# An adaLN block on one core: a written engine order up to the first h2, section steps one by one, four PSUM buffers for the first y, two warm-up matmuls

## The chip, the core and the metric

The kernel runs on one core of a Trainium2 chip. Its time is the device time of one execution in microseconds (us). A core has five engines that work side by side: TensorE (PE, matmul), VectorE (DVE), ScalarE (ACT), GpSimd (POOL) and SyncE (SP), which here only issues DMAs. Each engine works through its own instruction stream in order and waits on semaphores for the others. DMAs are issued from SP's stream, and one of them from ACT's.

## What is computed

x is (2, 2048, 1024) in float32: two batch entries of 2048 tokens with 1024 channels. From the reference, cut to what matters:

```python
mod = (_silu(L0_c) @ L0_wmod).reshape(2, 6, 1, -1)
sa, ca, ga, sb, cb, gb = (mod[:, 0], mod[:, 1], mod[:, 2], mod[:, 3], mod[:, 4], mod[:, 5])
ga = (2 * (ga >= 0) - 1) * jnp.maximum(jnp.abs(ga), 0.25)       # gb likewise
h = _layernorm(x, axis=-1) * (1 + ca) + sa
x = x + ga * attn(h)
h = _layernorm(x, axis=-1) * (1 + cb) + sb
return x + gb * ffn(h)

# attn: for each channel l a 2x2 softmax over the batch entries
q = jnp.transpose(x, (2, 0, 1))
prob = softmax(jnp.einsum('lnc,lmc->lnm', q, q) / scale)
return x + jnp.transpose(jnp.einsum('lnm,lmc->lnc', prob, q), (1, 2, 0))

# ffn: FF = 2752
y = (_silu(xf @ W_gate.T) * (xf @ W_up.T)) @ W_down.T
```

The attention needs, for each channel, sums over all 2048 tokens of z, of z squared and of the product of the two batch entries, where z is the normalised x. So there is one pass over all of x before anything else can begin.

## The kernel before

Tokens are worked in eight units of 256 (both batch entries together). Behind the pass over x each unit computes its y, the second layernorm (its result is called h2), the two projections to FF (gate and up, in pairs of 128-row blocks of FF), and the projection back. Float32 operands are split into a high and a low float16 part, and three of the four products are summed (`PARTS`). Units 1 to 7 form the projections as two-by-two block products in seven steps; unit 0 uses the plain product `gu_plain`, because its weights are split and written back to DRAM while it runs.

What comes before unit 0's first product, and some way into it, is the stretch that the change touches, from 0 to about 160 us. Its parts in order:

- **Modulation sections** 0 to 4 (`sa`, `ca`, `ga`, `sb`, `cb`). A section j has four loads of 1 MiB (`mod_load`, L158, DMA to `hbt`, `H` or `wt`; called w0 to w4 here), four steps of four matmuls (`mod_mul`, L165), a copy of the sum out of PSUM (`mod_row`, L171), a turn by four matmuls (`mod_turn`, L177) and a copy to SBUF (`mod_put`, L185/L187).
- **The pass over x**: `x_step` (L321) for eight steps of 256 tokens. It computes statistics and 1/std (`stats`, `root`, `dev`), z on DVE, POOL and ACT (`z_of`, L282), the products on POOL (L337), the squares on ACT (L318), and sums all of them by matmuls against a selector (`add`, L308, into the PSUM tile `sums`). It also transposes unit 0's z (`x_turn`, L299; `x_turned`, L304).
- `stat_rows` (L285 to L292) turns mean and 1/std of all tokens (PE, L289), copies them to SBUF (ACT, L291) and writes them to DRAM with a DMA that ACT issues (L292); unit 1's preparation reads them there.
- **The attention weights** alpha and beta from the sums (L1116 to L1149): a row copy (ACT), `pq` (PE, L1118), some thirty small DVE operations, an Exp and a dummy Sqrt on ACT, which loads the function table ahead of its use, and section 2.
- `first_y` (L648 to L662): for each of eight channel blocks q two activations `po` (ACT, L657), two products with z (DVE, L659), the addition to x (POOL for even q, DVE for odd, L660), and a matmul that sums over channels (`pmean`, L661). `po` is a PSUM tile of tag X, of which there are two.
- `first_dev` (L664 to L676): minus the mean (DVE, L668), squares (ACT, L671), sums `pvar` (PE, L673). `first_spread` (L679) is 1/std of the 128 x 128 result; `spread` (L683) lays it over all partitions (`pr`, L686).
- `first_h2` (L690 to L705): for each block two products with `pr` (DVE, L699), the high half (ACT, L701) and the low half (DVE), and between the blocks the four `split`s of pair 0's weights (L128: high half on POOL or ACT, low half on DVE). Pair 0's weights need their own power-of-two scale, from sums of squares (L115) by `pow2_from_sumsq` (L98) and `over_partitions` (L90).
- `gu_plain` (L739) for p = 0, 1, 2, ...: in p = 0 four warm-up matmuls (`WARM`, L749), then for each of four blocks i the products (L759).

Who sets the order: inside `tc.manual_schedule` an engine's instructions stand in the order of the text. SP is under it from the start to the last load of pair 0 (`in_order`). PE, DVE, ACT and POOL are under it (`in_text`) only for the pass over x, up to `in_text.close()` ahead of `mod_put(0, ...)`. What follows is placed by a scheduler that simulates time; `tc.issue_after(m)` keeps an instruction behind the marked one. The section steps are given such marks: section 2's stand after the sums of steps 6 and 7 and after pq, section 3's after the last `pmean`, section 4's after some of the `pvar` sums. Pair p's four float32 weight blocks are loaded by `Pair.load` (L412): pair 0 to `H`, pair 1 to `rot`, pair 2 to `big`. On SP's queue the order there is w2, w3, w4, pair 0, pair 1, pair 2 (four loads each).

Of the kernel before, what the change touches and what calls it, by code (L numbers as in the profile page):

```python
# [47 lines left out]
def adaln_kernel(ctx, tc, x, xT, wgp, wg20, wgl, wd, wd20, wd21, wmod, cT, out, nunits=NU):  # L48
# [41 lines left out]
    def over_partitions(col):  # L90

        pa = ps.tile([P, P], F32, tag="st", name="pa")
        mark["row"] = T.matmul(pa, col.broadcast_to([P, P]), ident, start=True, stop=True)
        a = small.tile([P, 1], F32, tag="p2a", name="p2a")
        V.tensor_reduce(a, pa, AX.X, ALU.max)
        return a


    def pow2_from_sumsq(col, s, inv):
        b = small.tile([P, 1], F32, tag="p2b", name="p2b")  # L100
        V.tensor_scalar(b, col, 1e-30, 1e38, ALU.max, ALU.min)
        a = over_partitions(b)
# [3 lines left out]
        V.tensor_single_scalar(inv.bitcast(I32), c, 0x1A000000, ALU.add)  # L106

# [9 lines left out]
    def rsqrt(dst, v, shape, pool, tag):  # L117

        s = pool if tag is None else pool.tile(shape, F32, tag=tag, name=tag + "s")
        first = S.activation(s, v, AF.Sqrt, bias=epst)  # L120
# [5 lines left out]
        return first, V.scalar_tensor_tensor(dst, s, 1.5, dst, ALU.add, ALU.mult)  # L126

    def split(dst_hi, dst_lo, src, s, on_pool=False):  # L128
        if on_pool:
            G.tensor_scalar(dst_hi, src, s, 0.0, ALU.mult, ALU.add)  # L130
        else:
            mark["hi"] = S.activation(dst_hi, src, AF.Copy, scale=s)  # L132
        return V.scalar_tensor_tensor(dst_lo, src, s, dst_hi, ALU.mult, ALU.subtract)  # L133
# [58 lines left out]
    def mod_section(j, slots, tag):  # L192
# [5 lines left out]
        mod_end(j, pm, tag)  # L198

    def section_of(j, wms, tag, after=None):  # L200

        pm = ps.tile([P, 512], F32, tag=tag, name=f"pm{j}")
        for kk, wm in enumerate(wms):
            with tc.issue_after(after[kk].ins) if after else ExitStack():
                mod_mul(pm, kk, wm)
        mod_end(j, pm, tag)
# [114 lines left out]
    def x_step(s):  # L321
# [11 lines left out]
        z_of(G, s, 1, 0)  # L333
        for n in range(2):
            z_of(S, s, n, 1)
        for c in range(NC):
            G.tensor_tensor(zz_at[c], z[c][0], z[c][1], ALU.mult)  # L337
# [4 lines left out]
        if s:  # L342
            turned[s - 1] = x_turn(z_first, s - 1)
            x_turned(zt, s - 1, turned[s - 1], S)
# [5 lines left out]
        for c in range(NC):  # L350
            add(s, 2, 2 * c, zz_at[c])
        for n in range(2):
            add(s, 1, 2 * n, zq[2 + n])
# [46 lines left out]
    class Pair:  # L400
# [15 lines left out]

        def scale(self):
            scale_of(self.sq, self.s, inv_gu[:, self.p:self.p + 1])
# [4 lines left out]
        def block(self, i, keep=True):  # L423
            w = self.w[i] = wtile(2 * self.n, "wq")
            split(w[:, 0:self.n], w[:, self.n:], self.q[i], self.s, on_pool=i % 2 == 1)
            if keep:
                self.store(i)
# [44 lines left out]
    WARM = 4  # L472
# [87 lines left out]
    def mod_b(mx1):  # L560

        b1 = mods[4]
        mx = small.tile([P, 1], F32, tag="mx", name="mx")
        V.tensor_reduce(mx, b1.rearrange("p k n -> p (k n)"), AX.X, ALU.max, apply_absolute_value=True)
        V.scalar_tensor_tensor(mx, mx, 33.0, mx1, ALU.mult, ALU.add)
        ma = over_partitions(mx)
        mark["mod_row"] = mark["row"]
# [4 lines left out]
        for n, src in (("b1", b1), ("sb", mods[3])):  # L572
# [75 lines left out]
    def first_y():  # L648
# [4 lines left out]
        for q in range(KB):  # L653
            po = ps.tile([P, 2, TU], F32, tag="X", name="po")
            o = tmp.tile([P, 2, TU], F32, tag="o", name="o", bufs=3) if q % 2 == 0 else po
            for n in range(2):
                mark["o"] = S.activation(po[:, n], zt[:, q, 0], AF.Identity, scale=alpha[:, n, 0, q:q + 1],  # L657
                                         bias=beta[:, n, q:q + 1])
                V.scalar_tensor_tensor(o[:, n], zt[:, q, 1], alpha[:, n, 1, q:q + 1], po[:, n], ALU.mult, ALU.add)  # L659
            (G if q % 2 == 0 else V).tensor_tensor(x0[:, q], o, x0[:, q], ALU.add)  # L660
            mark["y", q] = T.matmul(pm, ones, xf0[:, q], start=q == 0, stop=q == KB - 1)  # L661
        return pm  # L662

    def first_dev(pm):  # L664
        nb = 2 * TU // P
        pv = ps.tile([P, P], F32, tag="st", name="pvar")
        for q in range(KB):
# [3 lines left out]
            mark["sq"] = S.activation(sq, zf0[:, q], AF.Square)  # L671
            for j in range(nb):
                mark["var", q] = T.matmul(pv[32 * j:32 * j + 32], ones[:, 0:32], sq[:, j * P:(j + 1) * P], start=q == 0,  # L673
                                       stop=q == KB - 1, skip_group_check=True)
        mark["pv"] = pv

    def first_spread():
        rs = evp.tile([P, 512], F32, tag="ev", name="rs", bufs=3)[:, 0:P]
        mark["rv"], mark["rs"] = rsqrt(rs, mark["pv"], [P, P], ps.tile([P, P], F32, tag="X", name="rv"), None)  # L679
        return rs  # L680

    def spread(rs):
        nb = 2 * TU // P  # L683
        pr = ps.tile([P, 2 * TU], F32, tag="st", name="pr")
        for j in range(nb):
            mark["pr"] = T.matmul(pr[:, j * P:(j + 1) * P], ident[:, 32 * j:32 * j + 1].broadcast_to([P, P]), rs, start=j == 0,  # L686
                     stop=j == nb - 1, skip_group_check=True)
        return pr

    def first_h2(pr, blocks):  # L690
        h0 = hb0.rearrange("p h k (n c) -> p h k n c", n=2)
        b1s, sbs = mods["b1"], mods["sb"]
        with tc.manual_schedule(engines={mybir.EngineType.DVE}):
            for q in range(KB + 1):
                if q in blocks:
                    pairs[0].block(blocks[q], keep=False)
                for n in range(2):
                    if q < KB:
                        V.scalar_tensor_tensor(zt[:, q, n], zt[:, q, n], b1s[:, q, n:n + 1], pr[:, n * TU:(n + 1) * TU],  # L699
                                               ALU.mult, ALU.mult)  # L700
                        mark["h2"] = S.activation(h0[:, 0, q, n], zt[:, q, n], AF.Identity, bias=sbs[:, q, n:n + 1])  # L701
                for n in range(2):
# [528 lines left out]
```

## Time and profile before

| | us |
|---|---|
| median of 3 runs shown | 2629.77 (2627.58 to 2632.89) |
| the profiled execution | 2636.85 |
| its span, first to last instruction | 2635.1 |
| mean granted TensorE clock, of 1 | 0.992 |
| PE busy | 2563.4 (97%) |
| DVE busy | 1587.8 (60%) |
| ACT busy | 986.3 (37%) |
| POOL busy | 129.8 (5%) |

Points on the way to unit 0, from the timeline of the profiled execution:

| | at us |
|---|---|
| last `sums` matmul ends | 82.97 |
| stat DMA issued by ACT | 83.08 |
| beta ready, first `po` of first_y | 92.95, 92.98 |
| first `dev` of first_dev | 106.91 |
| first product of h2 | 124.09 |
| first matmul of `gu_plain`, p = 0, on PE | 127.56 |
| first matmul of p = 1 | 155.01 |
| first matmul of p = 2 | 178.26 |

How to read it: the page's table of slices cuts the span into 40 equal parts of 65.9 us and gives a digit of busy share for each engine. A row of the timeline gives start, duration, engine, line, operation, out<-in with shape, how many instructions follow one another without a gap, and in square brackets the engine's idle time before them and who ended it. A DMA's row on SP or ACT is its issue; the list of DMA issues gives the time from there to its landing. The granted clock is what the chip's throttle gave PE in a window.

### The profile page before, as it was taken

What the parts mean: (1) busy time and instruction counts of PE and PEld (TensorE: products, weight loads), DVE (VectorE), ACT (ScalarE), POOL (GpSimd) and SP (SyncE); (2) the same over time, 40 slices, a digit from 0 to 9 for tenths busy, and PEclk for the clock granted to TensorE, in tenths of its full rate; (3) what the DMA queues carried; (4) which work ended last, traced back from release to release, by engine and by line L of the source; (5) the groups of instructions that cost most, each with busy time, mean ns of one, the idle gap of its engine ahead of it and who ended that gap; (6) DMA issues with size and microseconds to landing.
All of it is one profiled execution on the core that took longest, in us unless ns stands there. A gap on an engine that the chain in (4) does not pass through costs nothing.

```text
span 2635.1 us, 50643 instructions
## 1 busy us (share of the span) xinstructions
PE 2563.4 (97%) x21673; PEld 2088.9 (79%) x21673; DVE 1587.8 (60%) x2648; ACT 986.3 (37%) x1502; POOL 129.8 (5%) x70
## 2 busy tenths in 40 slices
PE   7899999999999999999999999999999999999999
PEld 2344458788887888888887888878887888888887
DVE  8567779856676877583385625574284825622263
ACT  7677664433432444142242423233141513311230
POOL 6211100000000000000000000000000000000000
PEclk9999999999999999999999999999999999999999
DMA  9888765655568766576666666576666666656664
GB/s 391 315 307 309 309 245 187 228 201 192 171 202 295 249 232 203 195 239 200 194 208 219 208 200 200 197 229 201 191 214 211 210 202 201 202 192 203 202 199 152
DMA packets 159009, 586.61 MB, mean 223 GB/s; under 512 B 17216, under 2 KB 17280, under 8 KB 158784
## 3 DMA queue, kind: packets, MB, share of 16 engines
q1 hardware_dynamic: 158704, 583.35, 66.5%
q8 instruction: 169, 2.77, 0.4%
q14 instruction: 56, 0.46, 0.1%
q10 hardware_dynamic: 80, 0.03, 0.0%
HBM read 506.47 MB, written 76.84 MB: 221 GB/s over the span
## 4 chain that ended last, share of the span: by engine, by line
PE 79%; DMA 8%; DVE 7%; issue 3%; ACT 2%; POOL 0%; SPq 0%; DVEq 0%; ACTq 0%; POOLq 0%
PE pY L816 19%; PE pZ L816 12%; PE pX L816 12%; PE dY L1020 11%; PE dX L1020 8%; PE dZ L1020 7%; PE g L784 3%; PE pB L1046 3%; PE pl L854 1%; DMA wo<-dgu 1%; ACT junk L115 1%; DMA rot<-in_wgp_dram 1%; DVE bst L256 1%; DMA rot<-in_wd_dram 1%; PE g L759 1%
## 5 line engine op out<-in xcount | busy, mean ns | idle before, releaser
L816 PEld LDWEIGHTS <-w 128*128 128x128 f16 x8820 | 861.5, 98 | 109.6 <-DMA w<-dgu 6.9
L1020 PEld LDWEIGHTS <-wd 128*128 128x128 f16 x6720 | 658.3, 98 | 81.2 <-DMA wd<-dwd 4.0
L816 PE MATMUL pY<-hbt,w 128*128 128x256 f16 x3780 | 442.4, 273 | 0.0
L1020 PE MATMUL dY<-rot,wd 128*128 128x256 f16 x2880 | 320.3, 273 | 0.0
L816 PE MATMUL pX<-hbt,w 128*128 128x256 f16 x2520 | 300.6, 273 | 0.0
L816 PE MATMUL pZ<-hbt,w 128*128 128x256 f16 x2520 | 294.4, 273 | 5.8 <-DMA w<-dgu 5.0
L816 PEld LDWEIGHTS <-wo 128*128 128x128 f16 x2688 | 263.4, 98 | 39.4 <-DMA wo<-dgu 4.6
L132 ACT ACTIVATE rot<-H,sA 128x1024 f16<-128x1024 f32 (+1 forms) x168 | 162.7, 1001 | 239.7 <-PE dY L1020 129.8
L133 DVE SCALAR_TENSOR_TENSOR rot<-H,sA,rot 128x1024 f16<-128x1024 f32 (+1 forms) x168 | 182.2, 1100 | 80.3 <-ACT rot L132 80.0
L759 PE MATMUL g<-hbt,wq 128*128 128x512 f16 x1008 | 221.0, 379 | 2.7 <-ACT hbt L701 2.1
L1020 PE MATMUL dX<-rot,wd 128*128 128x256 f16 x1920 | 212.7, 273 | 3.7 <-DMA wd<-dwd 3.7
L1020 PE MATMUL dZ<-rot,wd 128*128 128x256 f16 x1920 | 213.5, 273 | 0.0
L833 DVE TENSOR_TENSOR ev<-pY,e 128x512 f32<-128x512 f32 (+1 forms) x72 | 47.8, 663 | 257.5 <-PE pY L816 256.5
L759 PEld LDWEIGHTS <-wq 128*128 128x128 f16 x1008 | 98.3, 98 | 120.7 <-issue 3.4
L115 ACT ACTIVATE junk<-H 128x1024 bf16<-128x1024 f32 (+1 forms) x100 | 98.7, 987 | 160.1 <-DVE H L843 139.1
L838 ACT ACTIVATE sil<-ev,inv_f 128x512 f32<-128x512 f32 (+1 forms) x72 | 50.4, 701 | 242.8 <-DVE ev L836 242.5
L816 PE MATMUL pY<-hbt,wo 128*128 128x256 f16 x1152 | 134.7, 273 | 2.6 <-DVE ev L833 2.4
L613 ACT ACTIVATE o<-big,beta,alpha 128x256 f32<-128x256 f32 x112 | 59.9, 591 | 203.4 <-DVE big L599 181.1
L824 DVE TENSOR_TENSOR ev<-pY,e 128x512 f32<-128x512 f32 (+1 forms) x72 | 47.7, 663 | 124.0 <-PE pY L816 124.0
L784 PE MATMUL g<-hbt,wo 128*128 128x256 f16 x960 | 108.0, 275 | 4.8 <-DMA wo<-dgu 4.8
L827 ACT COPY e<-pZ 128x512 f32<-128x512 f32 (+1 forms) x72 | 40.4, 562 | 190.1 <-PE pZ L816 189.9
L784 PEld LDWEIGHTS <-wo 128*128 128x128 f16 x960 | 94.3, 99 | 17.9 <-DMA wo<-dgu 5.7
(286 smaller groups left out, 2731.9 us busy)
## 6 DMA issues: line engine op xcount, KB each, us to landing
w<-dgu SPq DMA_DIRECT2D x350, 512.0 KB, 4.3
wd<-dwd SPq DMA_DIRECT2D x224, 640.0 KB, 4.0
wo<-dgu SPq DMA_DIRECT2D x85, 512.0 KB, 5.2
dgu<-wo SPq DMA_DIRECT2D x40, 512.0 KB, 4.1
rot<-in_wgp_dram SPq DMA_DIRECT2D x38, 512.0 KB, 6.0
dgu<-wq SPq DMA_DIRECT2D x35, 512.0 KB, 7.0
big<-in_wgp_dram SPq DMA_DIRECT2D x32, 512.0 KB, 8.0
out_dram<-big SPq DMA_DIRECT2D x30, 512.0 KB, 3.0
```

What stands on the lines that cost most here:

```text
L115: S.activation(jv, src, AF.Square, accum_out=col)
L132: mark["hi"] = S.activation(dst_hi, src, AF.Copy, scale=s)
L133: return V.scalar_tensor_tensor(dst_lo, src, s, dst_hi, ALU.mult, ALU.subtract)
L613: S.activation(o[:, n], z[:, q, 0], AF.Identity, scale=alpha[:, n, 0, q:q + 1], bias=beta[:, n, q:q + 1])
L759: T.matmul(pt[m, f].rearrange("p n c -> p (n c)"), w[:, wa, f, k], hb0[:, ha, 4 * kh + k], start=kh == 0 and k == 0 and j == 0, stop=kh == ...
L784: T.matmul(pt[m, f][:, n], w[:, wa, f, k], hb[:, ((1, 0), (2, 3))[kh][n], ha, k], start=kh == 0 and k == 0 and j == 0 and n == 0, stop=kh ...
L816: T.matmul(pt[a][:, f], w[:, wa, f, k], hb[:, i, ha, k], start=a not in seen, stop=k == 3 and j == 2, skip_group_check=True)
L824: V.tensor_tensor(u2, pt["Y"], e1, ALU.add)
L833: V.tensor_tensor(c22, pt["Y"], e1, ALU.add)
L838: S.activation(sr, u2, AF.Silu, scale=inv)
L1020: T.matmul(acc[a, h][:, j], w[:, k // 5, wa, k % 5], rot16[:, si % 2, ha, k], start=(a, h) not in seen, stop=k == KH - 1 and jj == 2, skip ...
L1046: T.matmul(pB, wt[0:n, k, wa, m, :], hp[0:n, k, ha, :], start=i == 0, stop=i == len(LAST) - 1)
```

## The change

The written order (`in_text`, and `in_order` for SP) is carried on from the pass over x to the end of the first h2. The code there is put into the order in which it is to run; the marks that stood in for it go. In detail:

- **Section steps one by one.** Section 0's four steps stand behind x-steps 2 and 3 as before; its turn moves from behind the pass to behind step 5, where section 1's first two steps stand too; section 1's last two stand inside step 6, ahead of its last four `add` matmuls (`between`). Section 2's four steps stand together behind pq. Section 3's stand behind q = 2, 3, 5 and 6 of first_y, with its row, turn and `mod_put` behind q = 7, followed by three of pair 0's sums of squares and section 4's first two steps; section 4's third and fourth step stand behind q = 2 and 4 of first_dev.
- **Step 7 of the pass**: the two z's of the second 128 tokens and the second product move from ACT and POOL to DVE; the transposes of blocks 6 and 7 stand both in it, ahead of the sums, and DVE copies them.
- **stat_rows** moves from behind the pass to just ahead of first_y.
- A dummy Exp ahead of pq loads the function table.
- **first_y**: `po` alternates between PSUM tags X and Y, four buffers instead of two.
- **first_h2** is cut in two halves, and pair 0's splits are cut into `high` (blocks 0, 1 and 3 on POOL, 2 on ACT) and `low` (DVE). DVE's order is: eight products of h2, low 0, eight lows of h2, eight products, low 1, eight lows, low 2, low 3. Pair 1's sums of squares and scale stand between and behind them, ahead of unit 0.
- **gu_plain**: `WARM` is 2 instead of 4, and in p = 0 the first two blocks' products are sorted by part (high by high, low by high, high by low); before it was the first block alone, sorted in the order of `PARTS`.

On SP's queue the order becomes: w2, w3's first two, pair 2's four (`big`), w3's last two, pair 0's four, w4's four, pair 1's four. ACT's stream gets the stat DMA directly ahead of the first `po`. Behind about 160 us the two builds have the same order but for some swaps.

The diff, cut to its core:

```diff
-    def x_step(s):
+    def x_step(s, between):
 
         z = [[z_tiles(s)[n][:, c] for n in range(2)] for c in range(NC)]
         if s == 0:
@@ -331,17 +335,18 @@
         if more:
             stats(s + 1, 1)
         z_of(G, s, 1, 0)
+
         for n in range(2):
-            z_of(S, s, n, 1)
+            z_of(S if more else V, s, n, 1)
         for c in range(NC):
-            G.tensor_tensor(zz_at[c], z[c][0], z[c][1], ALU.mult)
+            (G if more or c == 0 else V).tensor_tensor(zz_at[c], z[c][0], z[c][1], ALU.mult)
         zq = squares(s, 0)
         if more:
             root(s + 1)
         zq += squares(s, 1)
-        if s:
-            turned[s - 1] = x_turn(z_first, s - 1)
-            x_turned(zt, s - 1, turned[s - 1], S)
+        for k in range(s - 1, s + 1 - more):
+            if k >= 0:
+                x_turned(zt, k, x_turn(z_first, k), S if more else V)
         for c in range(NC):
             for n in range(2):
                 add(s, 0, 2 * n, z[c][n])
@@ -349,6 +354,7 @@
             add(s, 1, 2 * n, zq[n])
         for c in range(NC):
             add(s, 2, 2 * c, zz_at[c])
+        between()
         for n in range(2):
...
-    WARM = 4
+    WARM = 2
...
-    def first_y():
+    def first_y(between):
 
 
         x0 = xtile(0)
         pm = ps.tile([P, 2 * TU], F32, tag="st", name="pmean")
         for q in range(KB):
-            po = ps.tile([P, 2, TU], F32, tag="X", name="po")
+            po = ps.tile([P, 2, TU], F32, tag="XY"[q % 2], name="po")
             o = tmp.tile([P, 2, TU], F32, tag="o", name="o", bufs=3) if q % 2 == 0 else po
             for n in range(2):
-                mark["o"] = S.activation(po[:, n], zt[:, q, 0], AF.Identity, scale=alpha[:, n, 0, q:q + 1],
-                                         bias=beta[:, n, q:q + 1])
+                S.activation(po[:, n], zt[:, q, 0], AF.Identity, scale=alpha[:, n, 0, q:q + 1], bias=beta[:, n, q:q + 1])
                 V.scalar_tensor_tensor(o[:, n], zt[:, q, 1], alpha[:, n, 1, q:q + 1], po[:, n], ALU.mult, ALU.add)
             (G if q % 2 == 0 else V).tensor_tensor(x0[:, q], o, x0[:, q], ALU.add)
-            mark["y", q] = T.matmul(pm, ones, xf0[:, q], start=q == 0, stop=q == KB - 1)
+            T.matmul(pm, ones, xf0[:, q], start=q == 0, stop=q == KB - 1)
+            between(q)
         return pm
 
...
+    def first_h2(pr, qs):
+        for q in qs:
+            for n in range(2):
+                V.scalar_tensor_tensor(zt[:, q, n], zt[:, q, n], mods["b1"][:, q, n:n + 1], pr[:, n * TU:(n + 1) * TU],
+                                       ALU.mult, ALU.mult)
+                mark["h2"] = S.activation(h0[:, 0, q, n], zt[:, q, n], AF.Identity, bias=mods["sb"][:, q, n:n + 1])
+
+    def first_h2_low(qs):
+        for q in qs:
+            for n in range(2):
+                V.scalar_tensor_tensor(h0[:, 1, q, n], zt[:, q, n], mods["sb"][:, q, n:n + 1], h0[:, 0, q, n],
+                                       ALU.add, ALU.subtract)
...
-            if p == 0 and i == 0:
-                fkj.sort(key=lambda t: t[2])
+            if p == 0 and i < 2:
+                fkj.sort(key=lambda t: (0, 2, 1)[t[2]])
...
+    def steps_of(j, ws, kks):
+        if 0 in kks:
+            pms[j] = ps.tile([P, 512], F32, tag="st" if j < 2 else "Z", name=f"pm{j}")
+        for kk in kks:
+            mod_mul(pms[j], kk, ws[kk])
+
+    def row_of(j):
+        rows[j] = mod_row(j, pms[j])
+
+    def turn_of(j):
+        pts[j] = mod_turn(j, rows[j], "st" if j < 2 else "Z")
+
     for g in range(NU):
-        x_step(g)
+        def between():
+            if g == 6:
+                steps_of(1, w1, (2, 3))
+
+        x_step(g, between)
         if g + 4 < NU:
             x_load(g + 4)
         if g == 0:
             w0 += [mod_load(0, kk, slots[0:4]) for kk in (2, 3)]
-        for j, ws, g0 in ((0, w0, 2), (1, w1, 5)):
-            if g == g0:
-                pms[j] = ps.tile([P, 512], F32, tag="st", name=f"pm{j}")
-            if g0 <= g < g0 + 2:
-                for kk in (2 * (g - g0), 2 * (g - g0) + 1):
-                    mod_mul(pms[j], kk, ws[kk])
         if g in (2, 3):
+            steps_of(0, w0, (2 * g - 4, 2 * g - 3))
             w1 += [mod_load(1, kk, slots[0:4]) for kk in (2 * g - 4, 2 * g - 3)]
         if g == 4:
-            rows[0] = mod_row(0, pms[0])
-    x_turned(zt, KB - 1, x_turn(z_first, KB - 1), V)
-    in_text.close()
-    mod_put(0, mod_turn(0, rows[0], "st"))
-    mod_end(1, pms[1], "st")
-    stat_rows()
-
-
-    sa, ca = mods[0], mods[1]
+            row_of(0)
+        if g == 5:
+            turn_of(0)
+            steps_of(1, w1, (0, 1))
+    w2 = [mod_load(2, kk, slots_x) for kk in range(4)]
+    w3 = [mod_load(3, kk, slots[0:4]) for kk in range(4)]
+    pairs[0].load()
+    row_of(1)
+    turn_of(1)
+    mod_put(0, pts[0])
...
     row = evp.tile([P, 512], F32, tag="ev", name="srow", bufs=3)
     S.copy(row, sums_ps)
+    dummy = small.tile([P, 1], F32, tag="dum", name="dum", bufs=1)
+    S.activation(dummy, epst, AF.Exp)
     for b in range(4):
-        mark["pq"] = T.matmul(pq[:, b], row[:, b * P:(b + 1) * P], e10, start=b == 0, stop=b == 3, skip_group_check=True)
+        T.matmul(pq[:, b], row[:, b * P:(b + 1) * P], e10, start=b == 0, stop=b == 3, skip_group_check=True)
+    steps_of(2, w2, range(4))
+    w4 = [mod_load(4, kk, slots_x) for kk in range(4)]
+    pairs[1] = Pair(1, four(rot))
+    pairs[1].load()
...
-    ex = S.activation(Zz, Zz, AF.Exp, scale=float(NTOK) ** -0.5)
-    dummy = small.tile([P, 1], F32, tag="dum", name="dum", bufs=1)
-    with tc.issue_after(ex.ins):
-        S.activation(dummy, epst, AF.Sqrt)
+    S.activation(Zz, Zz, AF.Exp, scale=float(NTOK) ** -0.5)
+    row_of(2)
+    turn_of(2)
+    S.activation(dummy, epst, AF.Sqrt)
     V.tensor_tensor(mx, Zz[:, :, 0], Zz[:, :, 1], ALU.add)
     V.reciprocal(mx, mx)
     V.tensor_tensor(Zz, Zz, over_m(mx), ALU.mult)
     V.tensor_tensor(Zz, Zz, eye, ALU.add)
-    w2 = [mod_load(2, kk, slots_x) for kk in range(4)]
-    section_of(2, w2, "Z", [mark["sums", 6], mark["sums", 7], mark["pq"], mark["pq"]])
+    mod_put(2, pts[2])
     gate(mods[2])
     V.tensor_tensor(Zz, Zz, bn(mods[2]), ALU.mult)
     V.tensor_tensor(alpha, Zz, bm(a1), ALU.mult)
     V.tensor_tensor(us, Zz, bm(sa), ALU.mult)
     V.tensor_tensor(beta, us[:, :, 0], us[:, :, 1], ALU.add)
-    w3 = [mod_load(3, kk, slots[0:4]) for kk in range(4)]
-    w4 = [mod_load(4, kk, slots_x) for kk in range(4)]
-    pairs[0].load()
+    stat_rows()
+
+
+    def in_y(q):
+        if q in (2, 3, 5, 6):
+            steps_of(3, w3, [(2, 3, 5, 6).index(q)])
+        if q == KB - 1:
+            row_of(3)
+            turn_of(3)
+            mod_put(3, pts[3])
+            for i in (0, 2, 3):
+                pairs[0].sums(i)
+            steps_of(4, w4, (0, 1))
+
+    pm = first_y(in_y)
+    mx1 = mod_b_shift()
+
+    def in_dev(q):
+        if q in (2, 4):
+            steps_of(4, w4, [1 + q // 2])
+        if q == 5:
+            row_of(4)
+            turn_of(4)
+
+    pv = first_dev(pm, in_dev)
+    rs = evp.tile([P, 512], F32, tag="ev", name="rs", bufs=3)[:, 0:P]
+    rv = ps.tile([P, P], F32, tag="X", name="rv")
+    mod_put(4, pts[4])
+    pb = mod_b_start(mx1)
+    S.activation(rv, pv, AF.Sqrt, bias=epst)
+    pairs[0].sums(1)
+    V.reciprocal(rs, rv)
+    V.scalar_tensor_tensor(rv, pv, EPS, rs, ALU.add, ALU.mult)
+    mod_b_end(pb)
+    pp = pairs[0].scale_start()
+    V.scalar_tensor_tensor(rv, rv, -0.5, rs, ALU.mult, ALU.mult)
+    V.scalar_tensor_tensor(rs, rv, 1.5, rs, ALU.add, ALU.mult)
+    pairs[0].scale_end(pp)
+    for i in range(2):
+        pairs[0].high(i, True)
+    pr = spread(rs)
+    pairs[0].inv()
+    first_h2(pr, range(4))
+    pairs[0].low(0)
+    first_h2_low(range(4))
+    for i in (0, 2):
+        pairs[1].sums(i)
+    first_h2(pr, range(4, KB))
+    pairs[0].high(2, False)
+    pairs[0].high(3, True)
+    for i in (3, 1):
+        pairs[1].sums(i)
+    for i in range(1, 4):
+        pairs[0].low(i)
+        if i == 1:
+            first_h2_low(range(4, KB))
+    pairs[1].scale()
+    pairs[1].inv()
+    in_text.close()
     in_order.close()
-    ctx.enter_context(tc.issue_after(mark["load"].ins))
-    pm = first_y()
-    section_of(3, w3, "Z", [mark["y", KB - 1]] * 4)
-    first_dev(pm)
-    with tc.issue_after(mark["sq"].ins):
-        for i in (0, 2, 3, 1):
-            pairs[0].sums(i)
-    section_of(4, w4, "Z", [mark["var", 1], mark["var", 3], mark["var", 7], mark["var", 7]])
-    mod_b(mod_b_shift())
-    rs = first_spread()
-    pairs[0].scale()
-    pr = spread(rs)
-    with tc.issue_after(mark["rv"].ins):
-        first_h2(pr, {1: 0, 3: 1, 5: 2, 7: 3})
-    pairs[0].inv()
-    with tc.issue_after(mark["h2"].ins):
-        pairs[1] = Pair(1, four(rot))
-        pairs[1].load()
-        for i in range(4):
-            pairs[0].store(i)
-        for i in range(4):
-            pairs[1].sums(i)
-        pairs[1].scale()
-        pairs[1].inv()
+    ctx.enter_context(tc.issue_after(mark["h2"].ins))
+    for i in range(4):
+        pairs[0].store(i)
     for u in range(nunits):
         last = u + 1 == nunits
         unit(u, iter(()) if last else prep(u + 1), None if last else right_gu(V))
```

## The prediction, made before the changed kernel was run

> **What bounds the kernel now.** I read the table of slices first, then the clock and load of the first 150 us in windows of 5 us, then the waits of SP's queue, then each engine's timeline there.
>
> ```profile
> span 2635.1 us, 50643 instructions
> PE   7899999999999999999999999999999999999999
> PEclk9999999999999999999999999999999999999999
> DMA  9888765655568766576666666576666666656664
> ```
>
> One digit is 65.9 us. From the fourth on PE is full; only the first two to three leave something to win. The change reorders work before about 160 us, and the built order behind that differs in a handful of swaps. So I walk that stretch and ask how much earlier or later it hands over to unit 0's second pair (p=2), from where PE is busy without a pause. The profiled execution took 2636.85 us (span 2635.1); the median shown is 2629.77, 7.1 below. I sum on the profiled one and put the difference on the median. About 0.2% (5.3 us) is what a measurement of this kernel can tell from no change.
>
> ```profile
> 85.00:90.00 5.00, 4.29 (x36) 2.35 (x32) 1.80 (x14) 1.66 (x2) 0.00 (x0) 1.00 0.91 303
> 90.00:95.00 5.00, 0.01 (x1) 0.00 (x0) 3.46 (x17) 3.88 (x8) 0.00 (x0) 0.84 1.02 392
> 95.00:100.00 5.00, 3.41 (x4) 1.46 (x5) 4.52 (x10) 3.63 (x8) 2.54 (x2) 0.50 1.03 419
> 100.00:105.00 5.00, 4.39 (x10) 1.56 (x9) 3.77 (x8) 3.13 (x6) 2.54 (x2) 0.98 1.03 409
> ```
>
> (Window, length, then busy us of PE, PEld, DVE, ACT, POOL, granted clock, DMA share, GB/s.) Two things bear on the change: the loads fill the DMA engines (share 1.0) to 110 us, so a load moved back lands later; and PE, idle from 90.0 to 96.6, comes back at half clock (0.50).
>
> ```profile
> 83.08 0.51 ACTq L292 DMA_DIRECT2D stat<-hp  x1
> 92.98 2.81 ACT L657 ACTIVATE po<-big,beta,alpha 128x256 f32<-128x256 f32 x5 [1.02 <-DVE beta L1149]
> SPq L412 <- DMA hbt<-in_wmod_dram: 6.5, 4, 2.5
> ```
>
> SP's row says that loads of a pair waited four times, 6.5 us in all, for w4's loads to land. They write other buffers; what they share is a place eight DMAs on. In the trace the `rot` loads issue at 93.83, 97.11 and 99.19, just after w4's at 93.75, 96.63 and 99.18 landed; so do the next four after theirs. So in this program a DMA waits for the one eight before it. The stat DMA of L292 follows that rule and sits in ACT's own stream: at 83.08 its partner, w2's first load, had landed (68.82), and it cost nothing.
>
> **Part 1, the pass over x and the sums: gain.** Step 7 moves two z's and one product to DVE, whose rows are 0.81 (z) against 1.24 on ACT and 1.73 on POOL; the second POOL product (2.39, ends 78.85) leaves. hs, mod and eye work leave DVE's order ahead of step 7's dev, which comes 2.45 earlier. pt1 (0.95) and p16 (0.28) leave PE ahead of the last sums. PE then runs through from 65 us with 15.1 of work: the last sums end at 80.1 instead of 82.97.
>
> **Part 2, to alpha and beta: gain 3.9, then lost.** pq ends 2.1 after the sums instead of 3.4 (p16's and pz's place is free), and the Exp table load (1.28 at 88.92) is hidden by the dummy Exp. But w2's 16 matmuls (3.5) now follow pq in one go, then row 0.57 and turn 1.05; these end last. beta is ready at 89.1 instead of 92.95.
>
> **Part 3, the new wait: the largest term.** stat_rows now stands behind beta and just ahead of first_y. In the built order its DMA is number 49, and number 41 is w4's first load. That load is moved back too: before, it follows w3; after, the four `big` loads of pair 2 stand between w3's halves and pair 0's four loads ahead of w4. Durations on the full queue: 2.56 for 1 MiB, 1.28 for 512 KB. Before, w2's last lands at 76.48, w3's last at 87.53, w4's first at 91.22, pair 0's 100.46 to 104.30, pair 1's to 109.42, pair 2's to 114.44. After: w3's first two 82.4, pair 2's four 87.6, w3's other two 92.7, pair 0's four 97.8, **w4's first 100.4**. From the other end: pair 0's second landing, 101.74, less the 1.1 us gap before w4 that goes, is 100.6. I take 100.5. Behind the waiting DMA on ACT stand all 16 activations of first_y, and behind those DVE, POOL and PE. First po: 100.5 + 0.1 + issue 0.5 = 101.1, against 92.98: **8.1 later**. If the wait did not hold ACT: 89.1.
>
> **Part 4, first y.** Four PSUM buffers instead of two take out the gaps of DVE (0.64, 0.25, 0.15, 0.25, 0.64): 16 x 0.49 + 4 x 0.69 = 10.6, to 112.4, against 13.0 now. What is late next is PE: q=0 arrives over POOL (1.27) at 104.0; then eight pmean passes at 0.86 and four steps of w3, four matmuls each, also 0.86, which before ran behind the mean (106.80 to 110.4): 12 x 0.86 = 10.3.
>
> ```profile
> 95.26 1.27 POOL L660 TENSOR_TENSOR big<-o,big 128x512 f32<-128x512 f32 x1 [16.42 <-DVE o L659]
> 96.59 7.31 PE L661 MATMUL pmean<-big,ones 128*128 128x512 f32 x12 [6.57 <-POOL big L660]
> 106.91 4.87 DVE L668 TENSOR_TENSOR big<-big,pmean 128x512 f32<-128x512 f32 x8 [1.22 <-PE pmean L661]
> ```
>
> The 6.57 of idle on the PE row is followed by the clock of 0.50, and the first four records there last 0.85 instead of 0.43: +1.7. I add 1.7 to 2.4 and take 2.0: mean at 116.3. From below, nothing is possible only if PE did not idle, but after the change it idles from about 88 to 104, longer than before. [...]
>
> **Part 5, dev to the first h2: gain.** pt3 (turn 1.05) and mod3 with its maximum (0.57) now stand on DVE ahead of dev: dev starts at 117.9 (106.91 before, +11.0). ACT puts row3 and three sums of squares (1.18 each) ahead of the eight squares, to 119.55; the squares (0.52 each) and row4 (0.57) run to 125.3, held by w4's third step. Then var 0.3, square root 0.32, reciprocal 0.96, three products 0.3 each with the small operations between, rs 129.3, pr 2.07.
>
> ```profile
> 120.00:125.00 5.00, 4.26 (x16) 3.09 (x16) 2.93 (x18) 2.24 (x3) 2.01 (x2) 0.66 0.56 195
> 124.09 0.87 DVE L699 SCALAR_TENSOR_TENSOR big<-big,b1s,pr 128x256 f32<-128x256 f32 x2 [0.91 <-PE pr L686]
> ```
>
> First h2 at 131.65 against 124.09: from dev 13.7 instead of 17.1, since the sums of squares and row4 no longer stand between the squares and rs. **+7.6** here.
>
> **Part 6, unit 0's first pair.** The lows and h2's go 8 by 8 on DVE: 32 x 0.395 + 4 x 1.2 = 17.4, before 17.6. High blocks on POOL (1.12) instead of ACT (1.14): even. Two warm-up matmul pairs instead of four take 1.8 off 3.65; PE waits for DVE here, so this costs nothing at warm clock, and if the clock stayed half the bound is the 1.7 of the row above. PE ends the pair at 157.9 (151.04 before): +6.9. The second pair then saves: its scale is already done, so PE's pauses of 1.73 and of the `pa` waits up to 155.01 go, as does part of the 1.92 of a section step. First matmul of p=2: 182.6 instead of 178.26. **Sum: +4.3, with swaps +4.5**; 2636.85 + 4.5 = 2641.4, or 2634.3 on the median's scale.
>
> **The rivals.**
> - *No hold on ACT* (faster): the stat DMA passes, first_y starts at 89.1, and the 12.0 us come off everything up to h2: 4.5 - 12.0 = -7.5, **2622.3**. For it: in the trace of before this very DMA never waited. Against: its partner had landed by then, and the `rot` loads did wait. Chance 0.10.
> - *Clock* (slower): PE idles 16 us, so first_y and the tail stay at half clock longer. One window more costs 1.7 (+6.2, 2636); the whole of first_y cold costs 6.9, some of it under DVE (to 2641). It decides from 0.8 us beyond my sum. For it: 0.50 after 6.57 idle. Against: 0.98 in the next window. **2637.5**, chance 0.27.
> - *A later wait swallows the delay*: the chain of waits from 184 us on goes through the loads of `wd`. They issue only some 2 us later than before (158.95 against 156.95), so if that chain, not PE, sets unit 0, the delay shrinks to 0 to +2. For it: DMA is 8% of the chain that ended last. Against: PE is full in those slices. **2630.5**, chance 0.18.
> - *Forecast*: 2634.3 (own range 2631.5 to 2637), chance 0.45.
>
> **How the numbers follow.** Faster by over 0.2% is only the first rival: 0.10. The bound on the slow side is 2629.77 + 5.3 = 2635.1. Slower takes the clock's 0.27 but for 0.03, and 0.17 of the forecast's 0.45, whose upper end passes the bound: 0.41. Same: 0.49. The range leaves out the first rival and the cold extreme: 2626 to 2641.
>
> **What would show it.** In the profile after: the stat DMA on ACT's queue issues at 100 to 101 with w4's first load landing just ahead, and the first po follows within 1 us; DVE has no gap between the products of first y; PE's granted clock is 0.5 around 104; the first dev starts near 118, the first h2 near 132, p=2's first matmul near 182.6. If the first po stands near 89, part 3 is wrong; if p=2 starts at 182 and the end is not later, the third rival holds.

## The result, and the profile after

The changed kernel takes 2643.92 us (median of 5, 2639.84 to 2647.07) against 2630.87 (median of 5, 2627.58 to 2632.89) for the kernel before: ratio 1.0048, 95% interval 1.0033 to 1.0063. Measured a second time beside other kernels, 2643.53 against 2635.96, ratio 1.0028 (1.0017 to 1.0039). It is slower by 0.3 to 0.5%, 7 to 13 us. The forecast was 4.5 us slower, range 2626 to 2641: the time lies above the range.

The profiled execution took 2647.07 us. Its first lines and the table of slices:

```profile
span 2645.1 us, 50642 instructions
...
PE   7699999999999999999999999999999999999999
...
PEclk9899999999999999999999999999999999999999
DMA  9778875665467776676666666676666666656664
```

Only the second slice (66 to 132 us) is worse: PE 6 instead of 8, clock 8 instead of 9. From the third on PE is as full as before. So the place is where the forecast put it. The windows of the changed kernel there (window, length, busy us of PE, PEld, DVE, ACT, POOL, granted clock, DMA share, GB/s):

```profile
90.00:95.00 5.00, 0.00 (x0) 0.00 (x0) 0.00 (x0) 0.00 (x0) 0.00 (x0) 0.50 1.02 409
95.00:100.00 5.00, 0.00 (x0) 0.00 (x0) 0.00 (x0) 0.00 (x0) 0.00 (x0) 0.50 1.03 410
100.00:105.00 5.00, 0.47 (x1) 0.47 (x2) 2.14 (x5) 2.68 (x5) 1.26 (x1) 0.50 1.03 410
105.00:110.00 5.00, 4.92 (x6) 1.20 (x5) 3.41 (x7) 2.35 (x5) 1.27 (x1) 0.54 1.03 412
110.00:115.00 5.00, 5.00 (x27) 1.33 (x27) 3.31 (x7) 2.93 (x6) 1.49 (x2) 1.00 0.19 78
```

No engine works from 90 to 100; only loads move. From 104.5 on PE is full, and it gets half its clock until some 109.6 (0.54 is the mean from 105 to 110). The timeline of the changed kernel says why; here SP, DVE and ACT in the order of time (start, duration, engine, line, operation, and in brackets the idle time before it and who ended it):

```profile
69.49 3.16 SPq L418 DMA_DIRECT2D big<-in_wgp_dram  x4
86.34 6.70 SPq L170 DMA_DIRECT2D hbt<-in_wmod_dram  x4
88.87 0.17 DVE L1187 TENSOR_TENSOR beta<-us 128x16 f32<-128x16 f32 x1
100.38 0.51 ACTq L296 DMA_DIRECT2D stat<-hp  x1
100.94 0.57 ACT L679 ACTIVATE po<-big,beta,alpha 128x256 f32<-128x256 f32 x1 [13.22 <-DMA hbt<-in_wmod_dram]
```

beta is ready at 89.04. ACT stands still for 13.22 us, 11.9 of them behind beta, and the row names who let it go: a load of `hbt` from wmod, which is w4's first. By the trace it lands at 100.30, just ahead of 100.38, when the stat DMA issues. `big` (pair 2) had been queued at 69.49, ahead of w4. The same timeline further on, PE and DVE:

```profile
104.53 5.54 PE L682 MATMUL pmean<-big,ones 128*128 128x512 f32 x6 [17.24 <-POOL big L681]
110.00 1.07 PE L177 MATMUL pm<-H,csT 128*32 128x512 f32 x8
111.00 1.13 PE L682 MATMUL pmean<-big,ones 128*128 128x512 f32 x2
112.06 1.07 PE L177 MATMUL pm<-H,csT 128*32 128x512 f32 x8
113.05 1.98 PE L682 MATMUL pmean<-big,ones 128*128 128x512 f32 x4
...
118.16 1.13 PE L682 MATMUL pmean<-big,ones 128*128 128x512 f32 x2
119.12 0.95 PE L189 MATMUL pt<-sel,row 128*128 128x4 f32 x8
120.59 4.86 DVE L690 TENSOR_TENSOR big<-big,pmean 128x512 f32<-128x512 f32 x8
134.70 3.22 DVE L713 SCALAR_TENSOR_TENSOR big<-big,b1s,pr 128x256 f32<-128x256 f32 x8 [0.77 <-PE pr L704]
186.42 0.81 PE L775 MATMUL g<-hbt,wq 128*128 128x512 f16 x3
```

Two records of `pmean` make one pass (one 128 x 512 matmul in float32), eight records of `pm` one of section 3's steps. Three passes take from 104.53 to 110.00, 1.82 each. Then passes and steps alternate: a step takes 1.00 and a pass between two steps 1.06. PE stands idle for 0.15 us in all up to 119.28, the end of the mean (0.08 and 0.07 where a pass waits for POOL's addition): PE is the bound.

The difference to the kernel before, stage by stage, adds up to what p=2 shows:

| | before | after | change |
|---|---|---|---|
| first po at | 92.98 | 100.94 | +7.96 |
| first po to dev | 13.93 | 19.65 | +5.72 |
| dev to first h2 | 17.18 | 14.11 | -3.07 |
| first h2 to the end of the first pair | 26.95 | 26.22 | -0.73 |
| from there to p=2's first matmul | 27.22 | 25.50 | -1.72 |
| p=2's first matmul at | 178.26 | 186.42 | +8.16 |

At the last matmul the two profiles differ by 10.0; with the second profile of the changed kernel (e5 below) in place of the first it is 7.7 (8.2 at p=2).

### The profile page after: what moved, and what is told of

It is laid out like the page before. It is cut to its first block, busy times and chain, and to the rows that moved or that the text cites. A ratio compares the mean times of both kernels' runs of the same rounds, so it can differ in the third digit from the quotient of the medians.

```text
span 2645.1 us, 50642 instructions
## 1 busy us (share of the span) xinstructions
PE 2565.3 (97%) x21669; PEld 2085.5 (79%) x21669; DVE 1596.9 (60%) x2652; ACT 982.2 (37%) x1499; POOL 130.8 (5%) x70
## 4 chain that ended last, share of the span: by engine, by line
PE 78%; DMA 9%; DVE 7%; ACT 3%; issue 2%; POOL 0%; SPq 0%; DVEq 0%; ACTq 0%; POOLq 0%
PE pY L832 19%; PE pZ L832 12%; PE pX L832 12%; PE dY L1036 11%; PE dX L1036 8%; PE dZ L1036 7%; PE pB L1062 3%; PE g L800 2%; PE pl L870 2%; PE g L775 2%; DMA rot<-in_wgp_dram 1%; DVE bst L260 1%; DMA wo<-dgu 1%; ACT junk L124 1%; DMA out_dram<-big 1%
```

## The experiments

Twelve runs, each beside runs of the kernel before. e5 is the changed kernel itself, e9 alters the kernel before, the others alter the changed kernel. Times in us from their profiles; the ratio is to the kernel before, with its interval.

| run | first po | dev | first h2 | p=2 | ratio |
|---|---|---|---|---|---|
| before | 92.98 | 106.91 | 124.09 | 178.26 | 1 |
| changed | 100.94 | 120.59 | 134.70 | 186.42 | 1.0048 (1.0033 to 1.0063) |
| e1 | 95.80 | 115.44 | 129.54 | 181.26 | 1.0008 (0.9999 to 1.0017) |
| e2 | 90.55 | 110.21 | 124.15 | 175.87 | 0.9984 (0.9976 to 0.9993) |
| e3 | 101.03 | 120.71 | 134.82 | 186.54 | 1.0038 (1.0025 to 1.0051) |
| e4 | 88.97 | 107.19 | 121.21 | 172.94 | 0.9985 (0.9976 to 0.9994) |
| e5 | 101.00 | 120.65 | 134.76 | 186.48 | 1.0028 (1.0017 to 1.0039) |
| e6 | 100.96 | 118.80 | 132.91 | 184.63 | 1.0015 (1.0007 to 1.0024) |
| e7 | 101.20 | 120.85 | 134.96 | 186.68 | 1.0032 (1.0018 to 1.0046) |
| e8 | 91.60 | 105.68 | 119.03 | 170.76 | 0.9978 (0.9970 to 0.9987) |
| e9 | 93.05 | 106.97 | 123.64 | 177.80 | 0.9999 (0.9989 to 1.0009) |
| e10 | 89.09 | 102.91 | 116.36 | 168.73 | 0.9956 (0.9943 to 0.9970) |
| e11 | 89.40 | 103.21 | 115.74 | 167.47 | 0.9958 (0.9945 to 0.9972) |
| e12 | 100.97 | 120.62 | 134.72 | 186.45 | 1.0021 (1.0009 to 1.0033) |

**e1: pair 2's loads last on SP's queue.** In the kernel before a mark kept unit 0's loads behind pair 0's last; in the changed kernel the mark stands on an ACT instruction, and SP is free to issue them early.

```diff
     in_order.close()
+    ctx.enter_context(tc.issue_after(mark["load"].ins))
     ctx.enter_context(tc.issue_after(mark["h2"].ins))
```

> The changed kernel with pair 2's four loads held behind pair 1's on SP's queue, as before; nothing else moves ahead of unit 0. Theory A (the stat DMA waits for the load eight DMAs before it, w4's first, and holds ACT's stream): four loads of 1.28 us leave the queue ahead of w4, whose first load lands at 95.3 instead of 100.4; the stat DMA issues there, the first po stands at 95.8 instead of 100.94, and p=2's first matmul comes 5 us earlier, at 181.3; time 5 us below the changed kernel, about 2639. Rival B (the hold is not what counts; PE at half clock and later loads set the end of the tail): the first po moves, but dev and h2 by less than 2 us, time unchanged at 2643 to 2644.

ACT's timeline of e1:

```profile
95.24 0.51 ACTq L296 DMA_DIRECT2D stat<-hp  x1
95.80 0.57 ACT L679 ACTIVATE po<-big,beta,alpha 128x256 f32<-128x256 f32 x1 [7.83 <-DMA hbt<-in_wmod_dram]
```

Four loads of 1.28 us gone from in front of w4, and the hold is 5.1 shorter. Everything up to p=2 follows by 5.2. By the ratios the time falls by some 10 us against the changed kernel's first measurement (0.0040), more than the 5 expected, and by 5.3 against its second. Theory A holds, B falls.

**e2: the stat DMA on SP.**

```diff
-        S.dma_start(stat.rearrange("s w n (c p) -> (s w n c) p", p=P), rows)
+        Q.dma_start(stat.rearrange("s w n (c p) -> (s w n c) p", p=P), rows)
```

> The changed kernel with the stat DMA issued by SP behind pair 1's loads instead of by ACT. Theory A: the first po follows beta at once, at 89.1 instead of 100.94; first y keeps its pace of 3.85 us for two q, dev starts at 108.8 instead of 120.59, h2 at 122.9 instead of 134.70, p=2 at 174.6 instead of 186.42; time 11.8 us below the changed kernel, about 2632. Rival B: first y starts at 89 but the tail waits for w4's loads (the last lands at 108) and for PE at half clock, so h2 comes only about 5 us earlier and the time is about 2639.

The timeline of e2, ACT and DVE:

```profile
90.55 0.57 ACT L679 ACTIVATE po<-big,beta,alpha 128x256 f32<-128x256 f32 x1 [1.37 <-DVE beta L1187]
110.21 4.86 DVE L690 TENSOR_TENSOR big<-big,pmean 128x512 f32<-128x512 f32 x8
```

ACT's wait is now for beta. This profile runs 1.0 and then 1.5 behind the changed kernel's from about 10 us on, long before the edit (pq at 82.26 instead of 80.79); with that taken off, first po, dev and p=2 stand within 0.2 of the expectation. By the ratios the time is 16.8 us below the changed kernel's first measurement, 11.6 below its second (0.0044 of 2635). Without the hold the changed kernel is 0.16% faster than the one before, so it is the hold that makes it slower.

**e3: first y two q at a time.** Why did ACT wait for DVE between two halves of one `po` tile ([0.55 <-DVE o] in the changed kernel)? The scheduler had interleaved two tiles in the kernel before; the written order goes q by q. My theory after the result was that this sets first y.

```diff
-        for q in range(KB):
-            po = ps.tile([P, 2, TU], F32, tag="XY"[q % 2], name="po")
...
+        for q in range(0, KB, 2):
+            po = [ps.tile([P, 2, TU], F32, tag="XY"[i], name="po") for i in range(2)]
+            o = [tmp.tile([P, 2, TU], F32, tag="o", name="o", bufs=3), po[1]]
+            for n in range(2):
+                for i in range(2):
...
```

> The changed kernel with first y written for two q at a time: first halves of both po tiles, then second halves, on ACT and on DVE; the stat DMA stays where it is. Theory A2 (the pace of first y comes from ACT's second half of a po tile waiting for DVE's product with the first half of the same tile, which the scheduler's interleaved order hid before): DVE's gaps of 0.64 go, two q take about 2.8 us instead of 3.85, PE is the bound and the mean ends at 116.5 instead of 119.3; h2 and p=2 2.8 earlier, time about 2641. Rival C (half clock on PE sets first y, whatever DVE does): the mean still ends at 119, time 2643 to 2644.

The timeline of e3, PE and DVE:

```profile
104.63 5.49 PE L686 MATMUL pmean<-big,ones 128*128 128x512 f32 x6 [16.99 <-POOL big L685]
110.05 1.27 PE L177 MATMUL pm<-H,csT 128*32 128x512 f32 x8
120.71 4.86 DVE L694 TENSOR_TENSOR big<-big,pmean 128x512 f32<-128x512 f32 x8
```

Two q now take 2.7 us on ACT and DVE instead of 3.85, and dev does not move. The theory fell: PE, at half clock and then alternating, sets the mean. In this profile the clock came back 0.9 us later behind the first pass than in the changed kernel (110.5 against 109.56), which can hide a gain of 0.4 us, not one of 2.8.

**e4: both.**

> Both: stat DMA on SP and first y two q at a time. Theories A and A2: -11.8 and -2.8 add, p=2's first matmul at 171.8, time about 2629, 14.6 below the changed kernel and 1 to 2 below the kernel before. Rivals B and C: at least 2637.

dev comes at 107.19, 18.2 behind the first po instead of 19.65: of the 2.8 expected from the interleaving half appears, and none can be seen in the time (0.9985 against e2's 0.9984; the intervals are wider than 1.5 us).

**e5: the changed kernel again.**

> The changed kernel unaltered, a second time, beside the kernels of this call. All theories: first po at 100.9, dev at 120.6, p=2's first matmul at 186.4; 0.3 to 0.6% above the kernel before. It tells whether the part of the difference that comes after p=2 (10.2 us between the two profiles at the end, 8.2 at p=2) belongs to the change or to the runs.

The stages repeat within 0.1. The shift against the kernel before is 8.2 at p=2, 8.3 at 600 us and 7.7 at the end; in between it moves from 7.6 to 9.9 (in the first profile from 6.5 to 12.9). What the first profile had on top of p=2 was its own.

**e6: PE kept busy.** As e3, and ahead of first y:

```diff
+    fill = ps.tile([P, 2 * TU], F32, tag="Z", name="fill")
+    for k in range(18):
+        T.matmul(fill, ones, xf0[:, KB - 1], start=True, stop=True)
     pm = first_y(in_y)
```

> The changed kernel with first y two q at a time and the stat DMA still on ACT, and 18 matmuls of no use on PE between section 2's turn and first y, 0.86 us each, so that PE does not idle from 88 to 104. Theory C (the mean is set by PE: three passes at half clock and eight alternations of passes and section 3's steps at 1.0 instead of 0.86): granted clock 1.0 from 100 to 115, the first passes 0.86 to 1.0 instead of 1.85, the mean ends at about 116.5 instead of 119.3, dev at 117.8, time 2.9 below the changed kernel. Rival A2 (ACT and DVE set first y): dev stays at 120.7 and the time with it.

A window of e6 (columns as above), and its timeline, PE and DVE:

```profile
105.00:110.00 5.00, 4.25 (x16) 1.13 (x14) 4.44 (x10) 3.89 (x8) 2.54 (x2) 1.00 1.02 410
```

```profile
104.56 1.98 PE L686 MATMUL pmean<-big,ones 128*128 128x512 f32 x4 [1.53 <-POOL big L685]
107.30 1.13 PE L686 MATMUL pmean<-big,ones 128*128 128x512 f32 x2 [0.75 <-POOL big L685]
116.36 1.13 PE L686 MATMUL pmean<-big,ones 128*128 128x512 f32 x2
118.80 4.86 DVE L694 TENSOR_TENSOR big<-big,pmean 128x512 f32<-128x512 f32 x8
```

The clock is 1.00, the first two passes take 1.98 together, and dev comes 1.9 earlier than in e3, p=2 too. Theory C in kind; in size 1.9 of 2.9, since PE now waits for q (0.75). At full clock the eight passes and four steps still take 12.9 us (104.56 to 117.49), 12.2 without that wait, where the forecast had 10.3 before its addition for the clock: the alternation has a price of its own.

**e7: four warm-up matmuls** (`WARM = 4`).

> The changed kernel with four warm-up matmuls again. My forecast's step (PE waits for DVE in the first pair, so the warm-up costs nothing either way): PE ends the first pair and starts p=2 within 0.3 us of the changed kernel, no difference in time. Rival (the two left out were needed or in the way): with four, the first product comes 1.7 to 1.8 us later, at 139.3, and p=2 as much later; or the clock is at 1.0 sooner and p=2 up to 1 us earlier.

p=2 at 186.68 against 186.42 and 186.48. The first product starts 1.9 later (139.42 against 137.54), and from 146.3 on PE waits for h2 as in the changed kernel (there from 146.1). No difference.

**e8: section 3 ahead of first y**, with e2, e3 and e1.

```diff
     turn_of(2)
+    steps_of(3, w3, range(4))
     S.activation(dummy, epst, AF.Sqrt)
...
-        if q in (2, 3, 5, 6):
-            steps_of(3, w3, [(2, 3, 5, 6).index(q)])
+        if q == 3:
+            row_of(3)
+        if q == 5:
+            turn_of(3)
```

> Stat DMA on SP, first y two q at a time, section 3's four steps ahead of first y (its row, turn and copy behind q = 3, 5 and 7), pair 2's loads held behind pair 1's. Theory C: PE has only its eight passes in first y and no long idle, so DVE's pace sets the mean: dev at 101 to 102 instead of 107.2 (the kernel with the first two of these), h2 at 115 to 116, p=2 at 166 to 167; time about 10 us below the kernel before (ratio 0.996). Rival (the tail is set by w4's loads and later loads): dev at 102 but h2 not before 119, time as the kernel with the first two, ratio 0.9985.

The timeline of e8, ACT and PE, and one of its windows:

```profile
91.44 0.26 ACT L295 COPY hp<-p 64x128 f32<-64x128 f32 x1 [3.48 <-PE p L293]
95.20 7.83 PE L686 MATMUL pmean<-big,ones 128*128 128x512 f32 x12 [3.85 <-POOL big L685]
```

```profile
95.00:100.00 5.00, 4.80 (x6) 2.17 (x7) 4.44 (x11) 4.35 (x9) 2.08 (x3) 0.50 1.03 410
```

I had overlooked a wait: stat_rows' transpose stands on PE behind section 3's last step, and its copy on ACT ahead of the first po. The first po stands 2.2 behind beta (89.43), and PE idled for 3.85 and came back at 0.50. First h2 is still 2.2 earlier than in e4.

**e9: stat_rows late in the kernel before.**

```diff
-    stat_rows()
...
+    with tc.issue_after(sq_table.ins):
+        stat_rows()
     pm = first_y()
```

(`sq_table` is the dummy Sqrt.)

> The kernel before with stat_rows moved as the change has it, behind the dummy Sqrt on ACT and directly ahead of first y; its loads keep their order (w3, w4, pair 0, pair 1, pair 2), so the DMA eight before the stat DMA is w3's third load, landed at 85. Theory A (the place costs only through the partner): the stat DMA issues without a wait at 92 to 93, first po within 0.5 us of 92.98, time as before. Rival (a DMA ahead of first y on ACT's stream is the cost by itself): first po later by a microsecond or more, or the time above before by over 0.2%.

ACT's timeline of e9:

```profile
92.21 0.51 ACTq L292 DMA_DIRECT2D stat<-hp  x1
93.05 2.80 ACT L657 ACTIVATE po<-big,beta,alpha 128x256 f32<-128x256 f32 x5 [0.87 <-DVE beta L1148]
```

No wait, no cost. It takes both, the late place and a late partner.

**e10: all mended**: e8 with `stat_rows()` behind `pr = spread(rs)`.

> As e8, and stat_rows moved behind pr, so that its transpose on PE does not stand behind section 3's last step and ahead of the first po. Theory: first po at 89.3 instead of 91.6 as beta is ready, PE idles less than 2 us before the first pass and stays at full clock, dev at 101.5 to 102 instead of 105.7, h2 at 115, p=2 at 166; about 11 us below the kernel before, ratio 0.996. Rival (pair 0's loads and w4's, or the loads of unit 0, are late by then): dev moves but p=2 by less than 2 us, ratio 0.9978 as e8.

The timeline of e10, ACT, PE and DVE, and one of its windows:

```profile
89.09 3.16 ACT L680 ACTIVATE po<-big,beta,alpha 128x256 f32<-128x256 f32 x6 [1.52 <-DVE beta L1192]
92.69 1.98 PE L686 MATMUL pmean<-big,ones 128*128 128x512 f32 x4 [1.96 <-POOL big L685]
102.91 4.87 DVE L694 TENSOR_TENSOR big<-big,pmean 128x512 f32<-128x512 f32 x8 [1.38 <-PE pmean L686]
116.36 3.22 DVE L717 SCALAR_TENSOR_TENSOR big<-big,b1s,pr 128x256 f32<-128x256 f32 x8 [0.77 <-PE pr L708]
```

```profile
95.00:100.00 5.00, 3.83 (x9) 1.57 (x10) 4.44 (x10) 4.12 (x8) 2.09 (x3) 1.00 1.03 412
```

PE idles 1.96, keeps its clock, and waits for each pair of q. p=2 comes at 168.73, 9.5 ahead of the kernel before (166 expected), and the time is 0.44% below it by the ratio (the medians, 2626.85 and 2635.1, differ by 0.31%). This version beats both kernels.

**e11: e10 and PE fed behind pvar** (three passes as in e6, ahead of `mod_b_end`).

> As e10, with three matmuls of no use on PE (0.86 us each) behind pvar, where PE waits for the reciprocal and pr then runs at half clock (0.50 from 130 to 135 in the changed kernel). Theory: pr takes 1.0 instead of 1.95 and h2 comes 0.9 earlier than in e10; p=2 as much earlier, as DVE sets the first pair. Rival: the three passes end after rs and delay pr, no gain.

The timeline of e11, PE and DVE:

```profile
111.28 2.74 PE L1227 MATMUL fill<-big,ones 128*128 128x512 f32 x6
114.55 1.16 PE L708 MATMUL pr<-rs,ident 128*128 128x128 f32 x8
115.74 3.22 DVE L717 SCALAR_TENSOR_TENSOR big<-big,b1s,pr 128x256 f32<-128x256 f32 x8 [0.16 <-PE pr L708]
```

pr takes 1.16 instead of 1.95; first h2 is 0.6, p=2 1.3 earlier. In the time that is below what these runs resolve.

**e12: two PSUM buffers** (`tag="X"` for all `po` of the changed kernel).

> The changed kernel with the po tiles of first y all of tag X, two buffers as before instead of four. Theory: written q by q, ACT's second half of a tile waits for DVE's product with its first half, whatever the number of buffers, and PE sets the mean anyway, so dev stays at 120.6 and the time at the changed kernel's. Rival (the four buffers bring something, as my forecast had it): first y gets 1 to 2 us longer, dev at 122.

dev at 120.62: the four buffers bring nothing in this order.

## Why the prediction was wrong

- **Reading the slices**: PE is full from the third slice on, not from the fourth; nothing in the sum hangs on it.
- **Parts 1 and 2** (sums at 80.1, beta at 89.1): measured 79.9 and 89.04.
- **Part 3** (the stat DMA waits for w4's first load, 100.5; first po 101.1): 100.38 and 100.94. e1, e2 and e9 show the mechanism: 5 us with the loads, gone with the queue, absent with another partner.
- **Part 4** is the step that failed: PE's work in first y. It had eight passes and four steps at 0.86, 10.3 in all, and 2.0 for the clock, together 12.3: mean 116.3, dev 117.9. Measured: 14.75 (104.53 to 119.28), and dev at 120.59, 2.7 later. The mean began 0.5 later, as the second half of the first `po` waits for DVE. The larger miss is the price of 0.86, which holds in a row without a change of work (section 3's four steps behind the mean in the kernel before: the fourth starts at 109.40, 2.60 behind the first). The five passes and four steps from 110.00 on, at full clock, took 9.3, 1.03 each: 1.5 more than forecast, and e6 shows the same at full clock throughout (12.2 against 10.3). The clock is the smaller miss: the first three passes took 5.47 instead of 2.58. PE worked 5.0 us at half clock, which costs 2.5 where the forecast had 2.0; some 0.3 more is the third pass's wait for q=2, which POOL ends at 108.34. The 2.4 up to which the forecast let this term go, and the 2.0 that it took, were the author's estimate and stand in no trace or run; the row of before shows 1.7, the changed kernel 2.5. Its bound from below, no loss only if PE does not idle, does not hold either: e10 idles for 1.96 us and keeps 1.00. The gaps of DVE that four buffers were to take out became other gaps (0.64 at each second half), and e12 and e3 show that neither counted, because PE was the bound.
- **Part 5** (13.7 from dev to h2): 14.11, 0.4 more.
- **Part 6**: first pair 26.25, measured 26.22; half the warm-up costs nothing (e7). The second pair was to save 2.5 and saved 1.7.
- **The rivals.** "No hold" is out. The slower one, the clock, came only in part: 0.5 of the 3.8 by which p=2 was missed (186.42 against 182.6), which are 2.7 at dev, 0.4 from there to h2 and 0.8 in the second pair. It had the clock stay at half for longer because PE idles for longer, and priced one window more at 1.7. No run shows that step: behind nine idles there were 2.8 to 5.9 us at half clock, 4.9 behind the shortest (3.85, e8) and 4.8 behind the longest (17.45, e5). "A later wait swallows the delay" is out: in all twelve runs the shift at p=2 and the one that the ratio gives agree within 3 us.

Why did the row of before show 1.7? Full clock came back at 100.18 in the kernel before and at 109.56 in the changed one. Here are windows with a border there, two of the kernel before, up to it, and three of the changed one, two up to it and one behind (columns as above):

```profile
93.36:96.77 3.41, 0.18 (x1) 0.18 (x2) 2.99 (x6) 2.63 (x6) 1.27 (x1) 0.50 1.02 413
96.77:100.18 3.41, 3.41 (x5) 1.30 (x6) 2.97 (x7) 2.75 (x6) 1.27 (x1) 0.50 1.04 422
```

```profile
102.73:106.15 3.42, 1.62 (x2) 0.84 (x3) 2.47 (x5) 1.68 (x4) 1.26 (x1) 0.50 1.03 412
106.15:109.56 3.41, 3.33 (x5) 0.83 (x3) 2.37 (x5) 1.87 (x4) 1.27 (x1) 0.50 1.03 412
109.56:112.98 3.42, 3.42 (x20) 0.61 (x18) 2.10 (x5) 2.11 (x4) 1.27 (x1) 1.00 0.41 165
```

In the kernel before PE came back at 96.59 and had its clock 3.6 us later. In the changed kernel it came back at 104.53, and it took 5.0 us. So the row that I had weighed was close to the cheapest case: of nine such returns (below) only e4's, with 2.8, was cheaper. The length of the idle alone does not explain it: e9 has the same idle as the kernel before (6.56 against 6.57) and 4.9 us at half clock, e5 idles for 17.45 and has 4.8. What sets the moment at which full clock comes back was not shown.

What stays open: the time lies 9.6 us above the forecast (2643.92 against 2634.3). 3.8 of them had come by p=2, and 1.1 is the kernel before (2630.87 in the runs of the result, 2629.77 in those of the forecast); the other 4.7 stand in no stage of the change. The second measurement, 7.4 us slower, does not have them.

The forecast's direction was right, and so was its largest term, the hold. Its size failed by one term of the sum, the PE work of first y (12.3 us, measured 14.75), and by taking too narrow a range around it.

## What to carry to other kernels

Where a DMA waits for an earlier one, as the stat DMA here did for the one eight before it (issued at 100.38, w4's first load landed at 100.30), the cost of moving it is set by that partner and by whatever stands behind it on the engine that issues it; look up both in the built order, and put small late DMAs on the queue that nobody waits for (e2: first po at 90.55 instead of 100.94). Where a change lets PE idle, look up the granted clock behind the idle: here 3.85 to 17.45 us of idle were followed by 2.8 to 5.9 us at half clock, the shortest by 4.9 and the longest by 4.8. And price the work by rows in which the same kinds of matmul alternate (1.03 each here, 0.86 in a row). A mark that orders one engine may not order another's queue: the loads that slipped ahead of w4 did so because the mark had moved from a DMA to an ACT instruction.

## What the runs showed of the hardware

- Up to 150 us the granted clock was 0.50 from 18.26 to 25.09, from 93.36 to 100.18 and from 120.66 to 124.07 in the profile of the kernel before, and from 20.81 to 24.22, from 89.08 to 109.56 and from 130.03 to 136.86 in that of the changed kernel.
- In these nine runs PE came back from an idle to the first pass of the mean at half clock. The time at half clock from there on is, in the e runs, an estimate from the granted clock of their 5 us windows:

| run | idle, us | first pass at | at half clock from there, us |
|---|---|---|---|
| e8 | 3.85 | 95.20 | 4.9 |
| e4 | 5.39 | 92.58 | 2.8 |
| e9 | 6.56 | 96.64 | 4.9 |
| before | 6.57 | 96.59 | 3.6 |
| e3 | 16.99 | 104.63 | 5.9 |
| e12 | 17.23 | 104.57 | 5.3 |
| changed | 17.24 | 104.53 | 5.0 |
| e7 | 17.25 | 104.79 | 4.8 |
| e5 | 17.45 | 104.59 | 4.8 |

- After 1.96 us of idle the clock stayed at 1.00 in e10 (90 to 100) and was lost in e11 (0.91 from 90 to 95, 0.75 from 95 to 100), whose PE work up to there is the same. After 1.53 us it stayed at 1.00 in e6.
- Matmuls of no use, 15.62 us of them, kept the clock at 1.00 from 85 to 105 in e6, where the changed kernel had 0.50 from 90 to 105. Three passes of them shortened `pr` from 1.95 (e10) to 1.16 (e11); the clock from 110 to 115 was 0.70 there and 1.00 here.
